# Two role adapters in a row: first loads in chunks on two queues, the up phase's last results on VectorE, and the second layer's first x turned six pairs ahead

## The chip, the cores and the metric

The kernel runs on one core of a Trainium2 chip. A core has five engines that each work through their own list of instructions in order: PE (matrix products), VectorE (DVE), ScalarE (ACT), GpSimd (POOL) and SyncE (SP, which here only issues transfers). ACT can issue transfers too. The metric is the time of one execution on the device in microseconds, lower is better. Before the change it is 3129.63 us, the median of 3 runs (3129.15 to 3130.18).

## What is computed

There are 128 samples, each a matrix of 128 rows by 1024 values, and each has a role, which is one of three. Two layers follow one another. In each layer every sample passes through an adapter whose weights belong to its role:

```python
h = jnp.einsum('bsh,bhk->bsk', hidden_states, W_down[role]) + b_down[role][:, None, :]
h = jax.nn.gelu(h, approximate=False)
u = jnp.einsum('bsk,bkh->bsh', h, W_up[role]) + b_up[role][:, None, :]
y = hidden_states + u
mean = jnp.mean(y, axis=-1, keepdims=True)
var = jnp.mean(jnp.square(y - mean), axis=-1, keepdims=True)
yn = (y - mean) * jax.lax.rsqrt(var + LN_EPS)
return yn * gamma[role][:, None, :] + beta[role][:, None, :]
```

Here the width is 1024 and the inner width 512, all in float32. The second layer has weights of its own and the same roles.

## The kernel before

**Phases and items.** There are four phases: down and up of layer 0, then down and up of layer 1. A phase works through 64 items of two samples each. The samples are sorted on the chip by role, the commonest role first, so that 63 of the items ("pairs") have one role for both samples; one item takes the two samples left over. Below, an item is called by its number m in the phase's order, 0 to 63.

**Products.** A pair is one 2 by 2 block product by Winograd's scheme, with seven block products instead of eight. They use the weight blocks B11, B21, T2, T1, T3, B22, T4 in this order (`ORDER`); the T are differences of blocks. On the other side stand x (turned, so that its columns lie on the partitions) and three sums of its blocks, made by `winograd_sums` in four instructions (L418 to L421), nearly always on GpSimd. One block product takes PE about 1.72 us, a pair 12.06 us. The very first item multiplies plainly (`plain`), because its weights come in as plain rows. Every tensor that is multiplied is brought in by transfers of quarters (`quartered`) and turned by VectorE (`turn`, L547 for x; L656 for the up phases' h).

**The end of an up item.** `finish` normalizes each of the two samples: `squares` (ACT, then a power on GpSimd, L794), `scaled` (VectorE, L801), `stored` and `away`. `stored` multiplies by the deviation's inverse and adds beta: for sample 0 on ACT (L808) and GpSimd (L809), for sample 1 on VectorE (L811). `away` lets SP store the result to `mid` (L815) for the next layer.

**Order.** The order of each engine's instructions is fixed by a list of events with time keys. One item has 7 units (`SLOTS`), so item m of phase k has base 7 * (64 k + m); an event at base + 3.1 comes ahead of one at base + 5.4, and equal keys go in the order in which they were entered. Whatever an event issues, on any engine, stands on that engine's list in the order of the keys and is executed in that order. A key is not a time of execution. Consecutive items overlap: item m + 1 begins between the fourth and the fifth product of item m.

At the seam of the first up phase (k = 1) and the second down phase (k = 2) these keys count, given from the base of the second down phase's item 0:

| key | event | engine |
|---|---|---|
| -15, -14.9 | x of item 0, samples 0 and 1 (eight transfers) | SP |
| -10.6, -8.6 | `squares` of up item 61, samples 0 and 1 | ACT, GpSimd |
| -7.5 | `stored` of up item 61, sample 0 (L808, L809) | ACT, GpSimd |
| -6.9, -3.5 | turns of item 0; at the second one also its sums | VectorE, GpSimd |
| -5.2 | `away` of up item 61, sample 0 | SP |
| -4.9, -4.8 | x of item 1 (eight transfers) | SP |
| -4.4 | `away` of up item 61, sample 1 | SP |
| -4.25, -2.25, -0.25 | weights T2, T1, T3 of the down phase | SP |

The weight blocks live in eight slots of `wall`, each with three parts for the three places of roles. One slot is always spare, and the next phase's B11 goes there. The first three items of the second down phase keep their x in parts of weight blocks that are still empty (`among_weights`).

**The start.** `role_0`, the commonest role, is known first. Its down weights come as rows, 1 MiB by ACT's queue (`load_rows(0, ...)`) and 1 MiB by SP's (`load_rows(1, ...)`), with x of the first sample on SP between the two. Products with zeros (`zeros`, L262) are put between PE's small products of the sorting. `perm`, `role_of` and `place` are gathered by one small product each (`gathered`, L338). `first_sum` makes the differences T1 to T4 in place on VectorE (L171).

```python
at(-31, lambda: load_rows(0, 0, nc.scalar))
at(-30.5, load_bias_row)
at(-29, lambda: load_rows(1, 0, nc.sync))
at(-26, lambda: load_bias([0], nc.scalar))
at(0.3, lambda: subtract(slice(0, 1)))
for t, name in zip((-8.7, -2.5, 4.6, 4.7), ("T1", "T2", "T3", "T4")):
```

Of the kernel before, what the change touches and what calls it, by code (L numbers as in the profile page):

```python
# [13 lines left out]
ALU = mybir.AluOpType  # L14
# [12 lines left out]
def kernel(  # L27
# [117 lines left out]
    def load_rows(k, place, queue):  # L145
        role = reg(role_of, place, [queue.engine], R - 1) if place else reg(role_0, 0, [queue.engine], R - 1)
        src = layers[0][0][ds(role, 1)].rearrange("o (p m) c -> p (o m) c", p=P)
        queue.dma_start(rows_of[k][:, place].rearrange("p j h c -> p j (h c)"), src[:, ts(k, NQ)])

    first_weights = {  # L150
# [142 lines left out]

    zeros("bbbbbbbb")
    role_row, key = ps[:, 0:B], f32(R)
# [47 lines left out]
    perm = gathered("perm", wide, onehot)  # L343
    zeros("bbb")

# [11 lines left out]

    own_place, wide_place = f32(1), f32(SQ)
    counted(own_place, key, own_key, ALU.is_gt, ones_r)
    nc.vector.tensor_copy(wide_place, own_place.to_broadcast((P, SQ)))  # L360
    place = gathered("place", wide_place, onehot)
    zeros("bbbb")

# [9 lines left out]
    def set_places(item, engines):  # L373

        n = item.n
        if n < NFIRST:
            item.places = [0, 0]
        elif n < NPAIR:
            item.places = [reg(place, 2 * n, engines, R - 1)] * 2
        else:  # L380
            item.places = [reg(place, 2 * n + s, engines, R - 1) for s in range(2)]

# [15 lines left out]

    def quartered(t, srcs):

        for s, src in enumerate(srcs):
            n = src.shape[-1] // NQ
            for q in range(NQ):
                nc.sync.dma_start(  # L404
                    t[s][ts(q, SQ)], src[:, ts(q, n)].rearrange("(a t) c -> t a c", t=SQ)
                )
# [110 lines left out]
    class Down:  # L517
# [6 lines left out]

        def load(self):
            if self.among_weights:


                block = self.ph.weights[ORDER[self.m]].v
                self.xq = [block[:, 1 + s] for s in range(2)]  # L530
            else:
                self.xq = [flat("q", 4, f"xq{self.tag}_{s}", H) for s in range(2)]
            self.xq = [t.rearrange("p (a c) -> p a c", a=NQ) for t in self.xq]
            if self.early:
                quartered(self.xq[0:1], [self.early_x(0, ENG.SP)])
                return
            self.srcs = x_of(self.layer, self.n, ENG.SP)
            quartered(self.xq[0:1], self.srcs[0:1])

        def load_rest(self):  # L540
            quartered(self.xq[1:2], [self.early_x(1, ENG.SP)] if self.early else self.srcs[1:2])

# [17 lines left out]
        def prepare(self):  # L560
            self.begin_turns()
            self.sums = None
# [6 lines left out]
        def end_turns(self):  # L569
            if self.early:  # L570
                return
            self.turn(1)
            if self.n < NPAIR:
                winograd_sums(self.sums, self.a, nc.vector if self.ph is phases[0] and self.m == 1 else nc.gpsimd)

        def plain(self):
# [16 lines left out]
            steps = [(4 * s + 2 * k, lambda s=s, k=k: half(s, k)) for s in range(2) for k in range(2)]  # L593
            return steps + [(0.1 + k / 10, lambda k=k: self.turn(1, ts(k, NQ))) for k in range(2)]

# [27 lines left out]
    class Up:  # L623
# [150 lines left out]
        def finish(self):  # L774
            if self.last:
                return self.finish_last()
            steps = []
            for s in range(2):
                t = (10.4, 12.4)[s] if self.n < NPAIR else (10.9, 12.65)[s]
# [39 lines left out]

                steps += [(t, squares), (t + 1.3, scaled)]  # L820


# [21 lines left out]
    for k, ph in enumerate(phases):  # L844
        for m, n in enumerate(sequence):
# [4 lines left out]
            def load(box=box, ph=ph, n=n, kind=kind, m=m):  # L850
# [4 lines left out]
                item.before_last = ph is phases[-1] and m == NI - 2  # L855
                item.among_weights = ph is phases[2] and m < 3
                if m == left_over_at + 1:
                    item.SEED = -1.65
# [24 lines left out]
            if ph is phases[2] and m < 3:  # L883

                prepare = -6.9
                at(base - 3.5, lambda box=box: box["item"].end_turns())
            at(base + prepare, go)
        if k + 1 < len(phases):
# [44 lines left out]
            for name, (slot, free) in zip(ORDER, places):  # L933
# [21 lines left out]
    ph.bias, load_bias, subtract = bias_table(ph.vectors[0], 2)  # L955

    def load_bias_row():
        r = reg(role_0, 0, [ENG.Activation], R - 1)
        nc.scalar.dma_start(bias_row, ph.vectors[0][ds(r, 1), :])
# [58 lines left out]
```

## Time and profile before

The profile is of one execution that took 3130.06 us. Its span, from the first to the last instruction, is 3128.3 us, at a granted TensorE clock of 0.999 on average.

| engine | busy us | share of the span |
|---|---|---|
| PE (products) | 3112.7 | 99% |
| PEld (weight loads, beside the products) | 2047.8 | 65% |
| VectorE | 1975.8 | 63% |
| ScalarE | 1203.5 | 38% |
| GpSimd | 1777.3 | 57% |

Transfers moved 642.21 MB, 205 GB/s on average. A row of the timeline has the start and the length in us, the engine, the line, the operation, what it writes and reads, and how often; in brackets stands the idle time of the engine just before, and what ended it. `SPq` and `ACTq` are transfers issued by SP and ACT. A count in an `x8` is of instructions that ran one after another and are shown as one row. In a float32 product each block of weights takes two instructions.

The page's slices show how the load of VectorE grows in the up phases (each digit is a tenth of busy time in one fortieth of the span):

```profile
DVE  6554544544678777777864444444447877777777
```

The up phases are the slices 10 to 19 and 30 to 39, counted from 0.

### The profile page before, as it was taken

The page shows a single profiled execution, that of the slowest core. Times are in us where ns is not written, and L with a number is a line of the kernel's source. Part 1 is how long each engine was busy: PE and PEld are TensorE (multiplying, and loading weights), DVE is VectorE, ACT ScalarE, POOL GpSimd, SP SyncE. Part 2 cuts the span into 40 slices and gives each one's busy share as a digit, 9 for nine tenths or more (in the row PEclk, how much of TensorE's full clock was granted, in tenths as well). Part 3 has the DMA queues.
Part 4 walks back from the last instruction along what each step waited for, and adds up shares of the span by engine and source line. Part 5 has one row for each costly group of instructions (what it writes and reads, how often), then busy time and mean ns, then how long its engine had stood idle before and what let it go on. Part 6 is the DMA issues. An engine that isn't in the chain of part 4 may idle for free.

```text
span 3128.3 us, 42229 instructions
## 1 busy us (share of the span) xinstructions
PE 3112.7 (99%) x10796; PEld 2047.8 (65%) x10796; DVE 1975.8 (63%) x2807; ACT 1203.5 (38%) x2816; POOL 1777.3 (57%) x1391
## 2 busy tenths in 40 slices
PE   9999999999999999999999999999999999999999
PEld 6888888888544444444478888888884444444443
DVE  6554544544678777777864444444447877777777
ACT  1222222222454555454432222222224545454544
POOL 3545344444577767777654343444436777677775
PEclk9999999999999999999999999999999999999999
DMA  8778788876786565656687555555567765656564
GB/s 218 196 216 209 212 206 210 213 209 196 272 288 240 211 227 208 225 212 226 225 224 179 146 130 131 130 127 138 126 183 275 280 239 206 227 207 226 211 227 176
DMA packets 429735, 642.21 MB, mean 205 GB/s; under 512 B 35778, under 2 KB 305603, under 8 KB 428356
## 3 DMA queue, kind: packets, MB, share of 16 engines
q1 hardware_dynamic: 428930, 637.15, 66.2%
q8 instruction: 102, 1.67, 0.2%
q10 hardware_dynamic: 578, 2.36, 0.2%
q14 instruction: 125, 1.02, 0.1%
HBM read 405.02 MB, written 234.36 MB: 204 GB/s over the span
## 4 chain that ended last, share of the span: by engine, by line
PE 49%; POOL 1%; issue 0%; DMA 0%; SPq 0%; DVE 0%; ACT 0%; DVEq 0%; POOLq 0%; ACTq 0%
PE bu L427 14%; PE bd L427 14%; PE eu L427 7%; PE ed L427 7%; PE au L427 3%; PE ad L427 3%; POOL ou L809 0%; SPq L404 0%; DMA hd<-hd 0%; POOL Sd L420 0%; POOL Sd L418 0%; DMA wall<-mid 0%; POOL varu L794 0%; POOL xTd L419 0%; DVE ou L712 0%
## 5 line engine op out<-in xcount | busy, mean ns | idle before, releaser
L427 PE MATMUL bu<-wall,hTu 128*128 (+1 forms) x2048 | 921.3, 592 | 0.0
L547 DVE STREAM_TRANSPOSE xTd<-xqd 128x1024 f32<-128x1024 f32 (+1 forms) x252 | 504.9, 2071 | 350.7 <-PE bd L427 283.8
L427 PEld LDWEIGHTS bu<-wall,hTu 128*128 128x128 f32 x2048 | 389.1, 190 | 487.2 <-issue 456.6
L418 POOL TENSOR_TENSOR Sd<-xTd 128x512 f32<-128x512 f32 x124 | 159.7, 1288 | 790.4 <-DVE xTd L547 782.7
L794 POOL TENSOR_TENSOR varu<-varu,mhalf 128x1 f32<-128x1 f32 x254 | 329.6, 1298 | 393.8 <-ACT varu L793 393.8
L427 PE MATMUL bd<-wall,xTd 128*128 (+1 forms) x2064 | 487.1, 379 | 1.8 <-ACT bd L445 1.8
L427 PE MATMUL eu<-wall,hTu 128*128 (+1 forms) x1040 | 488.0, 592 | 0.0
L427 PE MATMUL bd<-wall,Sd 128*128 (+1 forms) x2000 | 472.8, 379 | 2.2 <-ACT hd L606 1.6
L427 PEld LDWEIGHTS bd<-wall,xTd 128*128 128x128 f32 x2064 | 392.0, 190 | 57.5 <-ACT bd L445 2.6
L427 PEld LDWEIGHTS bd<-wall,Sd 128*128 128x128 f32 x2000 | 379.7, 190 | 56.5 <-issue 2.6
L801 DVE SCALAR_TENSOR_TENSOR ou<-xu,meanu,tables 128x1024 f32<-128x1024 f32 x253 | 325.3, 1286 | 138.3 <-ACT ou L792 120.0
L611 ACT ACTIVATE hd<-hd 128x256 f32<-128x256 f32 x379 | 157.6, 416 | 534.5 <-DVE hd L610 534.4
L427 PEld LDWEIGHTS eu<-wall,hTu 128*128 128x128 f32 x1040 | 197.6, 190 | 247.4 <-issue 218.8
L788 ACT ACTIVATE partu<-statu 128x2 f32<-128x2 f32 x254 | 51.6, 203 | 728.7 <-DVE xu L690 728.7
L809 POOL TENSOR_TENSOR ou<-ou,tables 128x1024 f32<-128x1024 f32 x126 | 296.9, 2356 | 0.0
L792 ACT ACTIVATE ou<-xu,meanu 128x1024 f32<-128x1024 f32 x254 | 291.7, 1148 | 8.4
L681 DVE TENSOR_TENSOR xu<-bu,xu 128x512 f32<-128x512 f32 x256 | 176.1, 688 | 119.1 <-PE bu L427 119.1
L427 PE MATMUL ed<-wall,xTd 128*128 (+1 forms) x1064 | 251.0, 379 | 0.0
L418 POOL TENSOR_TENSOR hTu<-hTu 128x256 f32<-128x256 f32 x126 | 198.1, 1572 | 70.8 <-DVE hTu L656 49.0
L427 PE MATMUL au<-wall,hTu 128*128 (+1 forms) x504 | 236.8, 592 | 0.0
L427 PE MATMUL ed<-wall,Sd 128*128 (+1 forms) x1000 | 236.3, 379 | 0.1
L427 PE MATMUL ad<-wall,xTd 128*128 (+1 forms) x1000 | 236.2, 379 | 0.0
(135 smaller groups left out, 3383.1 us busy)
## 6 DMA issues: line engine op xcount, KB each, us to landing
xqd<-in_x_dram SPq DMA_DIRECT2D x512, 128.0 KB, 3.3
hd<-hd SPq DMA_DIRECT2D x256, 256.0 KB, 2.4
xu<-in_x_dram SPq DMA_DIRECT2D x128, 512.0 KB, 3.8
mid<-ou SPq DMA_DIRECT2D x128, 512.0 KB, 4.2
xu<-mid SPq DMA_DIRECT2D x128, 512.0 KB, 3.8
out_dram<-ou SPq DMA_DIRECT2D x125, 512.0 KB, 3.8
hqu<-hd SPq DMA_DIRECT2D x244, 256.0 KB, 5.0
xqd<-mid SPq DMA_DIRECT2D x488, 128.0 KB, 3.8
```

What stands on the lines that cost most here:

```text
L418: engine.tensor_tensor(dst[:, 1], a11, a21, ALU.subtract)
L427: nc.tensor.matmul(ps[:, 0:cols], a[:, j], w.rhs(r, j, cols), start=start and j == 0, stop=j == n - 1, skip_group_check=True,)
L547: nc.vector.transpose(self.a[:, s, chunks].rearrange("p j (t a) -> p j a t", t=SQ), self.xq[s].rearrange("p a (i j) -> p j a i", i=SQ)[:, ...
L611: nc.scalar.activation(y, y, AF.Gelu)
L681: nc.vector.tensor_tensor(y, ps, y, ALU.add)
L788: nc.scalar.mul(part, self.stat[:, s], -1.0 / H)
L792: nc.scalar.activation(box["o"], self.x[:, s], AF.Square, bias=m, accum_out=v)
L794: nc.gpsimd.tensor_tensor(v, v, mhalf[:, 0:1], ALU.pow)
L801: nc.vector.scalar_tensor_tensor(box["o"], self.x[:, s], box["m"][:, 0:1], row(self.ph.gamma), ALU.add, ALU.mult)
L809: nc.gpsimd.tensor_tensor(o, o, row(self.ph.beta), ALU.add)
```

## The change

Five things are done, in two groups.

At the start:
1. The first role's rows come in eight chunks of 256 KiB (`load_first_rows`), the first on ACT, then by turns on SP and ACT, the last on ACT; `first_role` keeps the role's register. x of the first sample goes half by SP and half by ACT, between the first and the second chunk.
2. `zeros` has 14 products instead of 8 behind the row of roles and 4 instead of 3 behind `perm`. `place` and the four zeros behind it leave the sorting: `own_places` goes to VectorE behind the first turns, and the gather comes behind the first half of the first sample's product. The turn of sample 1, `subtract` and T2 get later keys.

At the seam:

3. Item 0 of the second down phase is `ahead`. Its x is loaded one sample at a time (keys -42 and -31.5) into part 0 of the spare slot and turned into parts 1 and 2 (keys -34.8 and -24.3). The spare slot has B11's part 0 loaded later, as before; parts 1 and 2 of the weight blocks of this phase are loaded in another order, B11's last. Its sums get the key -8.4.
4. For up items 62 and 63 of layer 0 (`ending`) `stored` is on VectorE for both samples, at key t + 2.5 instead of t + 3.1.
5. For these two items `away` has the key t + 3.6 (before, t + 5.4 and t + 4.2).

```diff
+    def load_first_rows(j, queue):
+        src = rows_in_dram(first_role(queue.engine))
+        queue.dma_start(rows_of[j // NQ][:, 0, j % NQ].rearrange("p h c -> p (h c)"), src[:, j])
...
-    zeros("bbbbbbbb")
+    zeros("bbbbbbbbbbbbbb")
...
-    zeros("bbb")
+    zeros("bbbb")
...
-    own_place, wide_place = f32(1), f32(SQ)
-    counted(own_place, key, own_key, ALU.is_gt, ones_r)
-    nc.vector.tensor_copy(wide_place, own_place.to_broadcast((P, SQ)))
-    place = gathered("place", wide_place, onehot)
-    zeros("bbbb")
+    own_place, wide_place, place = f32(1), f32(SQ), []
+    def own_places():
+        counted(own_place, key, own_key, ALU.is_gt, ones_r)
+        nc.vector.tensor_copy(wide_place, own_place.to_broadcast((P, SQ)))
+    def places_in_order():
+        place.append(gathered("place", wide_place, onehot))
...
         def load(self):
+            if self.ahead:
+                self.srcs = x_of(self.layer, self.n, ENG.SP)
+                self.a = self.ph.weights[ORDER[0]].v[:, 1:3].rearrange("p s (j c) -> p s j c", c=P)
+                return
...
             if self.early:
-                quartered(self.xq[0:1], [self.early_x(0, ENG.SP)])
+                for k, queue in enumerate((nc.sync, nc.scalar)):
+                    quartered(self.xq[0:1], [self.early_x(0, queue.engine)], (2 * k, 2 * k + 1), queue)
...
+        def load_ahead(self, s):
+            self.xq = [self.ph.weights[ORDER[0]].v[:, 0].rearrange("p (a c) -> p a c", a=NQ)] * 2
+            quartered(self.xq[s : s + 1], self.srcs[s : s + 1])
...
-            return steps + [(0.1 + k / 10, lambda k=k: self.turn(1, ts(k, NQ))) for k in range(2)]
+            return steps + [(1.1 + k / 10, lambda k=k: self.turn(1, ts(k, NQ))) for k in range(2)]
...
+            ending = self.layer == 0 and self.m >= NI - 2
...
-                    if s == 0 and not self.before_last:
+                    if s == 0 and not self.before_last and not ending:
...
+                if ending:
+                    steps += [(t + 2.5, stored), (t + 3.6, away)]
+                    continue
...
+            elif m == 0:
+                first = rest = -43
+                for s in range(2):
+                    at(base - 42 + 10.5 * s, lambda box=box, s=s: box["item"].load_ahead(s))
+                    at(base - 34.8 + 10.5 * s, lambda box=box, s=s: box["item"].turn(s))
             else:
-                first = -15 if m == 0 else -11.9
+                first = -11.9
...
-                prepare = -6.9
-                at(base - 3.5, lambda box=box: box["item"].end_turns())
+                prepare = -6.9 if m else -8.5
+                at(base - 3.5 if m else base - 8.4, lambda box=box: box["item"].end_turns())
...
-                    later_on = SLOTS * (1 + 2 * ORDER.index(name) + k_)
+                    turn = ORDER.index(name) if nxt.up else (ORDER.index(name) - 1) % len(ORDER)
+                    later_on = SLOTS * (1 + 2 * turn + k_)
...
-    at(-31, lambda: load_rows(0, 0, nc.scalar))
+    at(-31, lambda: load_first_rows(0, nc.scalar))
     at(-30.5, load_bias_row)
-    at(-29, lambda: load_rows(1, 0, nc.sync))
+    for j in range(1, 7):
+        at(-29 + j / 10, lambda j=j: load_first_rows(j, nc.sync if j % 2 else nc.scalar))
+    at(-27, lambda: load_first_rows(7, nc.scalar))
     at(-26, lambda: load_bias([0], nc.scalar))
-    at(0.3, lambda: subtract(slice(0, 1)))
-    for t, name in zip((-8.7, -2.5, 4.6, 4.7), ("T1", "T2", "T3", "T4")):
+    at(-8.75, own_places)
+    at(1, places_in_order)
+    at(2.7, lambda: subtract(slice(0, 1)))
+    for t, name in zip((-8.7, 2.6, 4.6, 4.7), ("T1", "T2", "T3", "T4")):
```

More of the change, by code (lines that the diff above doesn't have):

```diff
@@ L1 @@
+import functools
 import heapq
@@ L145, in load_rows, with rows_in_dram @@
     def load_rows(k, place, queue):
-        role = reg(role_of, place, [queue.engine], R - 1) if place else reg(role_0, 0, [queue.engine], R - 1)
-        src = layers[0][0][ds(role, 1)].rearrange("o (p m) c -> p (o m) c", p=P)
+        src = rows_in_dram(reg(role_of, place, [queue.engine], R - 1))
         queue.dma_start(rows_of[k][:, place].rearrange("p j h c -> p j (h c)"), src[:, ts(k, NQ)])
+    def rows_in_dram(role):
+        return layers[0][0][ds(role, 1)].rearrange("o (p m) c -> p (o m) c", p=P)
+    def load_first_rows(j, queue):
+        src = rows_in_dram(first_role(queue.engine))
+        queue.dma_start(rows_of[j // NQ][:, 0, j % NQ].rearrange("p h c -> p (h c)"), src[:, j])
     first_weights = {
@@ L378, in set_places @@
         elif n < NPAIR:
-            item.places = [reg(place, 2 * n, engines, R - 1)] * 2
+            item.places = [reg(place[0], 2 * n, engines, R - 1)] * 2
         else:
-            item.places = [reg(place, 2 * n + s, engines, R - 1) for s in range(2)]
+            item.places = [reg(place[0], 2 * n + s, engines, R - 1) for s in range(2)]
     def samples(n, engine):
@@ L397, with quartered @@
     bias_row = first_rows[0:1, 0]
-    def quartered(t, srcs):
+    def quartered(t, srcs, quadrants=range(NQ), queue=nc.sync):
         for s, src in enumerate(srcs):
             n = src.shape[-1] // NQ
-            for q in range(NQ):
-                nc.sync.dma_start(
+            for q in quadrants:
+                queue.dma_start(
                     t[s][ts(q, SQ)], src[:, ts(q, n)].rearrange("(a t) c -> t a c", t=SQ)
@@ L538, in load @@
             quartered(self.xq[0:1], self.srcs[0:1])
+        def load_ahead(self, s):
+            self.xq = [self.ph.weights[ORDER[0]].v[:, 0].rearrange("p (a c) -> p a c", a=NQ)] * 2
+            quartered(self.xq[s : s + 1], self.srcs[s : s + 1])
         def load_rest(self):
+            if self.ahead:
+                return
             quartered(self.xq[1:2], [self.early_x(1, ENG.SP)] if self.early else self.srcs[1:2])
@@ L560, in prepare @@
         def prepare(self):
-            self.begin_turns()
+            if not self.ahead:
+                self.begin_turns()
             self.sums = None
@@ L571, in end_turns @@
                 return
-            self.turn(1)
+            if not self.ahead:
+                self.turn(1)
             if self.n < NPAIR:
@@ L856, in load @@
                 item.among_weights = ph is phases[2] and m < 3
+                item.ahead = ph is phases[2] and m == 0
                 if m == left_over_at + 1:
@@ L955, with first_role @@
     ph.bias, load_bias, subtract = bias_table(ph.vectors[0], 2)
+    @functools.cache
+    def first_role(engine):
+        return reg(role_0, 0, [engine], R - 1)
     def load_bias_row():
-        r = reg(role_0, 0, [ENG.Activation], R - 1)
-        nc.scalar.dma_start(bias_row, ph.vectors[0][ds(r, 1), :])
-    at(-31, lambda: load_rows(0, 0, nc.scalar))
+        nc.scalar.dma_start(bias_row, ph.vectors[0][ds(first_role(ENG.Activation), 1), :])
+    at(-31, lambda: load_first_rows(0, nc.scalar))
     at(-30.5, load_bias_row)
-    at(-29, lambda: load_rows(1, 0, nc.sync))
+    for j in range(1, 7):
+        at(-29 + j / 10, lambda j=j: load_first_rows(j, nc.sync if j % 2 else nc.scalar))
+    at(-27, lambda: load_first_rows(7, nc.scalar))
     at(-26, lambda: load_bias([0], nc.scalar))
-    at(0.3, lambda: subtract(slice(0, 1)))
-    for t, name in zip((-8.7, -2.5, 4.6, 4.7), ("T1", "T2", "T3", "T4")):
+    at(-8.75, own_places)
+    at(1, places_in_order)
+    at(2.7, lambda: subtract(slice(0, 1)))
+    for t, name in zip((-8.7, 2.6, 4.6, 4.7), ("T1", "T2", "T3", "T4")):
         at(t, lambda name=name: first_sum(name, 0))
```

## The prediction

> **What bounds the kernel now.** I read the page first. PE is busy 99% of a span of 3128.3 us and the chain that ended last is PE from end to end, so a gain can only come from the few places where PE waits. The list of waits gives PE some 10 us of them; laying PE's starts one after another (429 ns from one 512-column product to the next, 216 ns for 256 columns) puts nearly all the loss at three places: the start, the seam between the first up phase and the second down phase, and the tail, which the change leaves alone.
>
> The start, as stretches of the trace (length, PE, PEld, DVE, ACT, POOL busy, granted clock, DMA share, GB/s), then as a timeline:
>
> ```profile
> 12.29:15.70 3.41, 2.43 (x8) 0.83 (x6) 1.91 (x3) 0.00 (x0) 0.00 (x0) 1.00 0.98 329
> 15.70:19.11 3.41, 3.41 (x6) 1.34 (x5) 2.57 (x3) 0.00 (x0) 0.00 (x0) 0.50 1.08 233
> ...
> 13.84 2.13 DVE L547 STREAM_TRANSPOSE xTd<-xqd 128x512 f32<-128x512 f32 x2 [1.50 <-DMA xqd<-in_x_dram]
> 15.02 8.83 PE L587 MATMUL ad<-wall,xTd 128*128 128x512 f32 x16 [0.98 <-DVE xTd L547]
> 20.64 2.14 DVE L547 STREAM_TRANSPOSE xTd<-xqd 128x512 f32<-128x512 f32 x2 [2.33 <-DMA xqd<-in_x_dram]
> 24.84 7.13 PE L587 MATMUL ad<-wall,xTd 128*128 128x512 f32 x16
> ```
>
> PE has its first real product at 15.02 because sample 0's x lands only at 13.7; then it runs one stretch of 3.41 us at half clock. Starts spaced 0.53 to 0.85 us instead of 0.43 cost 1.8 us there.
>
> The seam, PE's timeline:
>
> ```profile
> 1568.16 1.97 PE L427 MATMUL bd<-wall,Sd 128*128 128x256 f32 x8 [0.49 <-DMA wall<-T]
> 1574.15 1.99 PE L427 MATMUL bd<-wall,xTd 128*128 128x256 f32 x8 [0.57 <-ACT bd L445]
> 1589.07 1.99 PE L427 MATMUL bd<-wall,xTd 128*128 128x256 f32 x8 [1.21 <-ACT bd L445]
> 1597.50 1.96 PE L427 MATMUL bd<-wall,Sd 128*128 128x256 f32 x8 [1.26 <-ACT hd L606]
> ```
>
> With three smaller ones these gaps sum to 5.9 us between 1567 and 1598. Behind those named ACT stands VectorE: it turns x four times between 1554 and 1576, and two adds of beta (L811) take 3.36 us instead of 1.25 because GpSimd's L809 runs at the same moment.
>
> GpSimd and SP's queue just before it are what I find decisive:
>
> ```profile
> 1552.58 1.32 POOL L794 TENSOR_TENSOR varu<-varu,mhalf 128x1 f32<-128x1 f32 x1 [2.45 <-ACT varu L793]
> 1553.87 2.38 POOL L809 TENSOR_TENSOR ou<-ou,tables 128x1024 f32<-128x1024 f32 x1
> 1561.33 0.55 POOL L794 TENSOR_TENSOR varu<-varu,mhalf 128x1 f32<-128x1 f32 x1 [5.08 <-ACT varu L793]
> ...
> 1550.52 0.32 SPq L937 DMA_DIRECT2D wall<-B  x1
> 1556.28 0.32 SPq L815 DMA_DIRECT2D mid<-ou  x1
> 1556.65 5.07 SPq L404 DMA_DIRECT2D wall<-mid  x8
> 1561.82 0.38 SPq L815 DMA_DIRECT2D mid<-ou  x1
> 1562.30 2.03 SPq L937 DMA_DIRECT2D wall<-T  x3
> ```
>
> SP stands still from 1550.84 until L809 of item 61, sample 0, ends (1556.25); only then go its store, item 1's eight x loads and the load of T2, which PE awaits at 1568.16. T2 is late already, by 0.5 us, and all of it hangs on that one GpSimd instruction.
>
> **The start.** Ahead of x stand 256 KiB of rows instead of 1 MiB; 0.79 MB less at the 0.36 MB/us that the trace moved from 8 to 10 us is 2.2 us. Two queues: the four issues take 2.15 us on SP (6.29 to 8.44); with half on ACT, behind a row chunk, the bias row and a register load, the last goes out near 7.9, 0.5 us sooner. A rule speaks against this part: the Trainium skill, "DMA: Bandwidth & Descriptors", section "Issuing engines are not separate DMA queues", says that the queues share the same engines, so a second one saves issue time alone. By it and by the row the queue is worth 0.5 us; what counts is the order of the bytes. x lands near 11.0, half a turn (1.07) makes PE ready at 12.3; the bias product (1.12 us, now right behind the last zeros) ends at 12.8. Real start 12.8 for 15.02: 2.2 us. PE has no hole ahead of it, since six more zeros (0.26 each) and one more fill it, so the half clock should go: 1.8 us. The place gather now lies inside the sample: 0.4 us back (L338, x2). Sum 3.6 us.
>
> What is late next: sample 1's x (turn at 20.64) has to be turned by 21.2; if it lands no sooner than now, its first half ends at 21.7, and 3.1 us remain. Item 2's turn (32.82 to 34.84, behind item 1's x, landed at 25.2, the sums and T3, T4) would let item 2 start at 34.95 for 38.71 now: a cap of 3.7. The row chunks have 2 KiB runs instead of 8 KiB. In the trace 8 KiB packets took 383 to 405 ns here; 2 KiB ones 150 ns (the bias table at 12 to 17 us) or 85 (300 to 400 us). Between, 110 ns: 2.1 MB take 7.0 us instead of some 6.4. DMA is full until 33 us, so this shifts all that follows. I take **3.4 us gained**, ends 0.5 (150 ns, the rival below) and 3.7. T2's moved difference (1.23 us) follows the turn on VectorE and is wanted only at item 1's third product.
>
> **x of the second down phase, six pairs ahead.** Its eight x loads go from one burst to two of four (some 2 us of SP each); hidden. The two turns (2.1 us each) leave 1554 and 1559 and go into pair items 59 and 60 on VectorE, which is 9.47 us busy per 12 there. How VectorE answers to an inserted 2 us the trace shows, at L916:
>
> ```profile
> 1504.17 0.69 DVE L690 SCALAR_TENSOR_TENSOR xu<-bu,xu 128x512 f32<-128x512 f32 x1 [0.19 <-PE bu L427]
> 1515.92 2.49 DVE L916 TENSOR_TENSOR first_rows<-first_rows 128x256 f32<-128x256 f32 x1
> 1518.33 0.68 DVE L690 SCALAR_TENSOR_TENSOR xu<-bu,xu 128x512 f32<-128x512 f32 x1
> 1530.07 0.68 DVE L690 SCALAR_TENSOR_TENSOR xu<-bu,xu 128x512 f32<-128x512 f32 x1
> ```
>
> PE's period is 12.06. The second L690 is 2.1 us late, the third still 1.8: a delay stays, since VectorE then waits 1.27 us twice per item for ACT. So the first turn leaves 1.8 us of lag, L916 adds its own, and the second turn, of which 1.27 us fill such a wait, 0.7. Lag against before: 2.4 us. At its height the second turn stands ahead of item 60's third result, now read at 1522.55: 1522.55 + 1.8 + 2.1 + 0.7 = 1527.1. PE wants that bank four slots of 1.72 us after the third product began (1519.3), at 1526.2: **1.0 us of new wait** with the hand-over (0 to 1.5).
>
> **Its sums on GpSimd.** Their key moves to -8.4. In issue order that is behind the power of item 61's sample 1 (-8.6) and ahead of L809 of item 61's sample 0 (-7.5). Four of 1.27 us with gaps are 5.35 us; beside VectorE's two-input work the four took 7.2 at 1561.85; I take 6.4, since the L811 and L801 in that stretch cross them. L809 then ends at 1556.25 + 2.4 + 6.4 + some 0.2 = 1565.3 instead of 1556.25. Item 61 is not among those whose end goes to VectorE, so its store really waits for it. SP's order behind it is unchanged: store, eight loads, store, T2. T2 lands 11.8 us after that store now (1556.25 to 1568.05), so at 1577.1. PE reaches that product at 1567.5 + 1.0 = 1568.5 and waits **8.6 us** instead of 0.65; with fewer waits of SP among the eight loads (4.15 us in the next burst, not 5.07) 7.7. I take 8.2; with no lag at all 5.9.
>
> Such a hole has a price after it. The same skill, "TensorE: Matmul & The Clock Gate", Part 1, says that an idle window of about 3.4 us halves the clock until a busy one has passed. One window at half is 1.7 us; by the row above a window 71% busy still led to one at 0.50, so it may be 2.7 us. I take **1.7**.
>
> **The end of the up phase on VectorE.** Items 62 and 63 lose two ACT multiplies (1.13) and two L809 (2.36); VectorE gains two of 1.25 us, but its two L811 fall from 3.36 to 1.25: -1.7 us. With the turns gone and PE held at T2, VectorE and ACT are ahead afterwards: the waits at 1574 to 1597 go. The whole 5.9 us is taken off, since the T2 wait is counted anew.
>
> **Sum:** -3.4 + 1.0 + 8.2 + 1.7 - 5.9 = +1.6 us. The sum is made against the profiled execution (3130.06: its span and 1.8 us around); the median shown is 0.4 below it. 3129.63 + 1.6 = **3131.2**. Its own range, from the ends (no lag: -1.3; start 2.5, wait 9.3, clock 2.7: +5): 3127 to 3135.
>
> **Rivals.** (1) T2 is not held: the sums slip in before 1553 or SP is not the gate. Then -3.4 - 5.9 + 1.0 + some 0.6 of the old T2 wait = -7.7: 3122. For it: GpSimd idles 5 us at 1556. Against: each engine keeps its order, and SP stands exactly until L809. Chance 0.15.
> (2) Slower: the 2 KiB rows at 150 ns. 2.1 MB take 9.6 us instead of 6.4, item 1's x lands at 28.4, item 2's turn ends near 38 and the start is worth 0.5 us; with the rest unchanged +4.5: 3134. It decides once a 2 KiB packet takes over about 120 ns. Chance 0.2.
> (3) The wait does not cool the clock and there is no lag: 3128 or less; inside the first case.
> The forecast has 0.65. That the change does something else than it says I see no way to; the order of issue is fixed by its keys.
>
> A measurement of this kernel tells about 0.2%, 6.3 us, from no change: below 3123.4 is faster, above 3135.9 slower. Faster 0.14, nearly all of rival 1; slower 0.18 from the upper part of rival 2 and of the main case; same 0.68. Range 3124 to 3136.5.
>
> **What would show it.** With the start's gain all times are some 3.4 us earlier. Right: first L587 product near 12.8, no clock of 0.50 before 20 us; GpSimd with four L418 to L421 between L794 and the last L809 of the phase; SP's mid store some 9 us later; one PE wait of 6 to 9 us for wall<-T and a slice at half clock behind it; no other wait above 0.3 us up to 1600; PE's hole near 1523. Wrong: T2 issued near 1559, or the first item 1 product later than 29.

## The result, and the profile after

The changed kernel takes 3138.5 us (median of 9 runs, eight of them at 3137.0 to 3139.1), the kernel before beside it 3129.71 (9 runs, 3128.08 to 3131.95): **slower by 0.28%** (ratio 1.0028, 95% interval 1.0019 to 1.0036). The ninth run took 3216.4 us, at a granted clock of 0.972 where the others have 0.997 or 0.998, and is left out of the ratio. Forecast were 3131.2 us and a range up to 3136.5. The profiled execution took 3139.03 us with a span of 3137.2, 8.9 longer than before.

Two places differ. The first rows below are windows of the changed kernel: start and end, length, then busy time of PE, PEld, DVE, ACT, POOL (counts in brackets), granted clock, share of the DMA engines in use and GB/s.

```profile
11.60:15.01 3.41, 1.81 (x5) 0.73 (x5) 1.86 (x2) 0.00 (x0) 0.00 (x0) 1.00 1.05 331
15.01:18.43 3.42, 3.42 (x6) 1.34 (x5) 1.69 (x5) 0.00 (x0) 0.00 (x0) 0.50 1.06 249
...
1571.48:1574.90 3.42, 0.00 (x0) 0.00 (x0) 2.06 (x2) 0.00 (x0) 0.00 (x0) 1.00 1.06 253
1574.90:1578.31 3.41, 0.00 (x0) 0.00 (x0) 3.41 (x8) 1.17 (x5) 0.00 (x0) 0.50 1.05 393
1578.31:1581.72 3.41, 2.65 (x6) 2.19 (x7) 2.50 (x2) 1.48 (x3) 1.82 (x2) 0.50 0.98 368
1581.72:1585.14 3.42, 3.42 (x6) 1.69 (x5) 0.00 (x0) 0.37 (x1) 3.25 (x3) 0.50 1.06 349
1585.14:1588.55 3.41, 3.41 (x16) 2.81 (x15) 2.08 (x4) 1.92 (x5) 1.27 (x1) 1.00 1.14 218
```

The half clock of the start is still there, and the seam has got one of its own, three windows long. The timeline of VectorE and PE at the start, after the change (the code has moved: L571 is the turn, L613 and L438 are products, L456 copies the bias into a bank, L707 and L716 read results, L179 makes the differences):

```profile
13.15 2.12 DVE L571 STREAM_TRANSPOSE xTd<-xqd 128x512 f32<-128x512 f32 x2 [2.03 <-DMA xqd<-in_x_dram]
14.34 5.40 PE L613 MATMUL ad<-wall,xTd 128*128 128x512 f32 x8 [1.59 <-DVE xTd L571]
21.95 2.13 DVE L571 STREAM_TRANSPOSE xTd<-xqd 128x512 f32<-128x512 f32 x2 [1.57 <-DMA xqd<-in_x_dram]
24.68 7.13 PE L613 MATMUL ad<-wall,xTd 128*128 128x512 f32 x16
39.94 2.00 PE L438 MATMUL bd<-wall,xTd 128*128 128x256 f32 x8 [1.21 <-ACT bd L456]
```

x of sample 0 is there 0.7 us sooner, that of sample 1 is 1.3 us later (21.95 for 20.64), and item 2 begins at 39.94 for 38.71. The start loses 1.2 us where 3.4 were to be won.

The seam, first PE, then GpSimd (L822 the power, L429 to L432 the sums, L837 the beta add), VectorE and SP's queue (L843 the store to `mid`, L415 item 1's x, L974 weights):

```profile
1528.25 1.98 PE L438 MATMUL bu<-wall,hTu 128*128 x4 [0.47 <-DVE xu L707]
...
1569.50 1.96 PE L438 MATMUL eu<-wall,hTu 128*128 x4 [1.01 <-DVE xu L707]
1579.07 3.75 PE L438 MATMUL bd<-wall,Sd 128*128 128x256 f32 x8 [7.62 <-DMA wall<-T]
```

```profile
1556.16 1.32 POOL L822 TENSOR_TENSOR varu<-varu,mhalf 128x1 f32<-128x1 f32 x1 [2.44 <-ACT varu L821]
1557.46 1.26 POOL L429 TENSOR_TENSOR Sd<-wall 128x512 f32<-128x512 f32 x1
...
1563.59 3.33 POOL L837 TENSOR_TENSOR ou<-ou,tables 128x1024 f32<-128x1024 f32 x1
1566.88 2.28 POOL L822 TENSOR_TENSOR varu<-varu,mhalf 128x1 f32<-128x1 f32 x2
```

```profile
1567.47 1.28 DVE L839 SCALAR_TENSOR_TENSOR ou<-ou,varu,tables 128x1024 f32<-128x1024 f32 x1 [2.14 <-POOL varu L822]
1568.67 0.68 DVE L707 TENSOR_TENSOR xu<-eu,xu 128x512 f32<-128x512 f32 x1
```

```profile
1553.05 0.32 SPq L974 DMA_DIRECT2D wall<-B  x1
1566.95 0.32 SPq L843 DMA_DIRECT2D mid<-ou  x1
1567.32 4.16 SPq L415 DMA_DIRECT2D wall<-mid  x8
1571.58 0.38 SPq L843 DMA_DIRECT2D mid<-ou  x1
1572.05 2.36 SPq L974 DMA_DIRECT2D wall<-T  x3
```

Read upwards: PE waits 7.62 us for T2; SP issues T2 at 1572.05, because it stood from 1553.4 until the store of item 61 at 1566.95; that store waits for L837, and L837 stands behind the four sums. The other waits after 1573 are gone. The wait of 1.01 us ahead of it is new: VectorE stands at item 62's `stored` (L839) for the power on GpSimd, which is behind L837 too, and PE's result is read behind that.

Below, a kernel's **offset** is how much later than in the kernel before PE starts one and the same product, trace against trace. Of the changed kernel it is +1.33 us at 75 us (all of the start) and +8.74 at 1606 us, and it stays there to the end. So in this trace the start costs 1.33 us and the seam 7.41.

### The profile page after: what moved, and what is told of

Same layout as the page of the kernel before. It is cut to its first block, busy times and chain, and to the rows that moved or that the text cites. A ratio compares the mean times of both kernels' runs of the same rounds, so it can differ in the third digit from the quotient of the medians.

```text
span 3137.2 us, 42253 instructions
## 1 busy us (share of the span) xinstructions
PE 3115.6 (99%) x10799; PEld 2049.8 (65%) x10799; DVE 1974.9 (63%) x2809; ACT 1201.9 (38%) x2814; POOL 1772.1 (56%) x1389
## 3 DMA queue, kind: packets, MB, share of 16 engines
q8 instruction: 102, 1.67, 0.2%
## 5 line engine op out<-in xcount | busy, mean ns | idle before, releaser
L438 PE MATMUL bu<-wall,hTu 128*128 (+1 forms) x2048 | 922.9, 593 | 0.7 <-DVE xu L707 0.7
L571 DVE STREAM_TRANSPOSE xTd<-xqd 128x1024 f32<-128x1024 f32 (+1 forms) x252 | 505.9, 2072 | 350.5 <-PE bd L438 282.9
L438 PEld LDWEIGHTS bu<-wall,hTu 128*128 128x128 f32 x2048 | 389.5, 190 | 489.3 <-issue 455.2
L429 POOL TENSOR_TENSOR Sd<-xTd 128x512 f32<-128x512 f32 x123 | 157.5, 1280 | 795.1 <-DVE xTd L571 795.1
L822 POOL TENSOR_TENSOR varu<-varu,mhalf 128x1 f32<-128x1 f32 x254 | 330.2, 1300 | 398.9 <-ACT varu L821 398.7
L438 PE MATMUL eu<-wall,hTu 128*128 (+1 forms) x1040 | 488.1, 592 | 1.0 <-DVE xu L707 1.0
L438 PE MATMUL bd<-wall,xTd 128*128 (+1 forms) x2048 | 483.3, 379 | 1.2 <-ACT bd L456 1.2
L438 PE MATMUL bd<-wall,Sd 128*128 (+1 forms) x2000 | 474.3, 380 | 7.6 <-DMA wall<-T 7.6
L438 PEld LDWEIGHTS bd<-wall,xTd 128*128 128x128 f32 x2048 | 389.0, 190 | 55.7 <-ACT bd L456 1.6
L438 PEld LDWEIGHTS bd<-wall,Sd 128*128 128x128 f32 x2000 | 381.0, 191 | 61.3 <-issue 9.4
L438 PEld LDWEIGHTS eu<-wall,hTu 128*128 128x128 f32 x1040 | 197.5, 190 | 248.8 <-issue 218.8
L837 POOL TENSOR_TENSOR ou<-ou,tables 128x1024 f32<-128x1024 f32 x124 | 293.2, 2364 | 0.0
L707 DVE TENSOR_TENSOR xu<-bu,xu 128x512 f32<-128x512 f32 x256 | 175.9, 687 | 118.4 <-PE bu L438 118.4
L438 PE MATMUL ed<-wall,xTd 128*128 (+1 forms) x1056 | 249.1, 379 | 0.0
L429 POOL TENSOR_TENSOR hTu<-hTu 128x256 f32<-128x256 f32 x126 | 197.7, 1569 | 72.8 <-DVE hTu L682 60.6
L438 PE MATMUL au<-wall,hTu 128*128 (+1 forms) x504 | 236.8, 592 | 0.0
L438 PE MATMUL ed<-wall,Sd 128*128 (+1 forms) x1000 | 236.2, 379 | 0.0
L438 PE MATMUL ad<-wall,xTd 128*128 (+1 forms) x992 | 234.3, 379 | 0.0
```

Source lines behind the costliest of these rows:

```text
L429: engine.tensor_tensor(dst[:, 1], a11, a21, ALU.subtract)
L438: nc.tensor.matmul(ps[:, 0:cols], a[:, j], w.rhs(r, j, cols), start=start and j == 0, stop=j == n - 1, skip_group_check=True,)
L571: nc.vector.transpose(self.a[:, s, chunks].rearrange("p j (t a) -> p j a t", t=SQ), self.xq[s].rearrange("p a (i j) -> p j a i", i=SQ)[:, ...
L707: nc.vector.tensor_tensor(y, ps, y, ALU.add)
L822: nc.gpsimd.tensor_tensor(v, v, mhalf[:, 0:1], ALU.pow)
L837: nc.gpsimd.tensor_tensor(o, o, row(self.ph.beta), ALU.add)
```

## The experiments

All ratios are against the kernel before, run on the same chip in the same rounds (median 3128.7 to 3129.2 us). "Seam" is PE's lost time between 1490 and 1620 us: 5.9 us before, 13.3 in the changed kernel.

### Which half of the change costs what

`e1_start_alone` has parts 1 and 2 of the change on the kernel before, `e2_seam_alone` parts 3 to 5.

> Only the start's part of the change, on the kernel before. By PE's starts the start costs 1.2 us (item 2's first product at 39.94 for 38.71), so 3131 us. Rival, that start and seam need each other (the earlier or later start shifts what happens at the seam): then anything away from +1.2 by over 2 us. My forecast's own term was -3.4 us, 3126.

> Only the seam's part, on the kernel before. By PE's starts waits and half clock at the seam grow from 5.9 to 13.3 us, so +7.4 us, 3137 us, with the one wait of some 7.7 us for wall<-T. If the seam is worth less without the new start, the two parts meet somewhere.

Measured: the start alone 3133.02 us (1.0014, 1.0007 to 1.0020), offset +2.35 at 75 us; the seam alone 3134.93 us (1.0019, 1.0011 to 1.0027), seam 11.8 us, offset +5.93 at the end. Each is a loss of its own, and the start is no gain that something later takes back. By the medians the halves cost 4.2 and 6.1 us, the whole change 8.8; the start alone is 2 us above what was expected for it. The start does not cost the same in every execution: the five traces with exactly this start have offsets at 75 us of +1.33 (the changed kernel), +1.75 (e4 below), +2.35 (e1), +3.93 (e10) and +4.18 (e3). In the last two item 2 waits 2.2 us instead of 1.21, and another window at half clock follows, from 41.3 and 42.0 us.

### What holds T2 at the seam

Three ways to free it, each on the changed kernel. In `e3_sums_behind` the sums go behind the beta add on GpSimd:

```diff
-                at(base - 3.5 if m else base - 8.4, lambda box=box: box["item"].end_turns())
+                at(base - 3.5 if m else base - 7.4, lambda box=box: box["item"].end_turns())
```

In `e4_weights_first` T2, T1 and T3 are loaded ahead of item 61's store:

```diff
-                at(base + free + 0.75, lambda f=load_part: f(0))
+                early = {"T2": 1.7, "T1": 1.71, "T3": 1.72} if k == 1 else {}
+                at(base + early.get(name, free + 0.75), lambda f=load_part: f(0))
```

In `e10_store_behind_weights` only item 61's stores move, behind those three loads; the sums keep their place:

```diff
-                    steps.append((t + (5.4, 4.2)[s], away))
+                    late = self.layer == 0 and self.m == NI - 3
+                    steps.append((20.8 + s / 20 if late else t + (5.4, 4.2)[s], away))
```

> The changed kernel with the four sums of item 0 behind L809 of item 61 on GpSimd (key -7.4 for -8.4). Theory of the queue: L809 ends some 5.6 us sooner, SP's store, x of item 1 and T2 with it; PE waits about 2 us for T2 in place of 7.8 and the clock stays full: 9 to 10 us less than the changed kernel, 3128 to 3129.5. Rival, the lag of VectorE from the two turns is what costs: the wait stays over 6 us, under 3 us gained.

> The changed kernel with the sums where it has them (L809 just as late), but T2, T1 and T3 are put on SP's queue ahead of item 61's store and of item 1's x. Theory of the queue: T2 lands near 1560, no wait for wall<-T, no half clock; what is left are the waits at 1527, 1533 and 1568 and perhaps 1 us for item 1's x: 8.5 to 10.5 us less than the changed kernel, 3128 to 3130. Rival, the lateness of GpSimd itself (sums, L809, the powers behind it)[...] holds PE: at most 3 us gained.

> The changed kernel with nothing moved but SP's two stores of up item 61, from keys -5.2 and -4.4 to -0.2 and -0.15: behind the loads of T2, T1 and T3. The sums still stand ahead of the beta add on GpSimd, which still ends near 1567. If SP's queue behind that store is what holds T2 (my theory): T2 is issued before 1563, PE's wait of 7.6 us for it and the half clock behind it go, the lag of 1.2 us and the wait of 1.25 us at 1568 stay, and the time falls by 6 to 10 us against the changed kernel (some 3130). If GpSimd's delay holds PE in another way (the sums themselves, the buffers of the results): a wait of several us stays at the seam and the time stays above 3135.

Measured: e3 3132.82 us (1.0012, 1.0003 to 1.0021), seam 5.6 us. e4 3135.77 (1.0021, 1.0014 to 1.0029), seam 8.1. e10 3132.79 (1.0011, 1.0004 to 1.0018), seam 5.6. PE and SP in e10:

```profile
1572.14 1.96 PE L438 MATMUL eu<-wall,hTu 128*128 x4 [1.02 <-DVE xu L707]
1573.93 1.89 PE L438 MATMUL bd<-wall,Sd 128*128 128x256 f32 x8
1576.98 1.98 PE L438 MATMUL bu<-wall,hTu 128*128 x4 [1.16 <-DVE xu L716]
...
1562.96 3.34 SPq L975 DMA_DIRECT2D wall<-T  x3
1569.59 2.15 SPq L843 DMA_DIRECT2D mid<-ou  x3
```

The beta add (1566.23 to 1569.57) is as late as ever and the store too, but T2 is issued at 1562.96, its product has no wait, and the half clock is gone with the wait. So SP's queue is the gate, as was argued. What comes then is the next thing in line: waits of 1.16 us at 1577 and 1.41 at 1591 for VectorE, which the long wait had covered. With T2 free the seam is thus 5.6 us, hardly under the 5.9 before. In time e3 and e10 are 5.7 us below the changed kernel, less than the 9 to 10 and the 6 to 10 that were expected, although their seams are 7.7 us shorter: their starts cost 2.9 and 2.6 us more in the traces.

e4 did not show this, because its edit made a wait of its own: T2's slot still had a reader, the second product of item 63 (`au`). The load is entered ahead of that product, so the product waits for it.

```profile
1560.17 3.55 PE L438 MATMUL au<-wall,hTu 128*128 x4 [5.00 <-DMA wall<-T]
```

### The lag of VectorE, and the end of the up phase

On the kernel before, with the old start: `e5_ahead_without_ending` has x six pairs ahead and its sums at -7.4, but `ending` off; `e6_ending_without_ahead` has the three `ending` hunks of `finish` alone; `e7_turns_in_waits` has the whole seam part with the sums at -7.4 and other keys for loads and turns. First e5's line (beside that of e3), then e7's:

```diff
-            ending = self.layer == 0 and self.m >= NI - 2
+            ending = False
```

```diff
-                first = rest = -43
+                first = rest = -46
...
-                    at(base - 42 + 10.5 * s, lambda box=box, s=s: box["item"].load_ahead(s))
-                    at(base - 34.8 + 10.5 * s, lambda box=box, s=s: box["item"].turn(s))
+                    at(base - 45.5 + 7.5 * s, lambda box=box, s=s: box["item"].load_ahead(s))
+                    at(base - 38.3 + 7 * s, lambda box=box, s=s: box["item"].turn(s))
```

> Old start. x of the second down phase turned ahead, its sums behind L809 of item 61, but items 62 and 63 end as before (sample 0 on ACT and GpSimd). If it is the turns in the crowded stretch that made the old 5.9 us of waits, they fall to some 1.2 us at 1526 and 1532 and about 3 us at the seam: 3128, 1 us less than before. If the end of the items made them[...], they stay near 5.9 and the 1.2 come on top: 3130.

> The kernel before with nothing but the new end of items 62 and 63 (sample 0's last step on VectorE). [...]both L811 fall from 3.36 to about 1.3 us, VectorE is some 1.7 us less behind and the waits at 1574 to 1597 fall from 5.2 to 3 us: 3127. If only the turns matter, no change: 3129. If the new step waits for GpSimd's power and holds what stands behind it on VectorE, as at 1567 in the changed kernel, slower by 1 to 2 us.

> Old start, the whole seam part with the sums behind L809, and the two turns put where VectorE waits for ACT anyway (keys -38.3 and -31.3, in two items ahead of L916's). Theory of the lag: VectorE is not behind when L916 comes, so the waits of 1.2 us at 1526 and 1532 are gone, L809 ends 2 us sooner than with the turns at -34.8 and -24.3, and the seam has 3 to 4.5 us of waits: 3126.5 to 3128.5. Rival, any 4 us more on VectorE in the up phase come out as lag: the waits stay, 3129.5 to 3130.5.

Measured: e5 3128.49 us (0.9998, 0.9990 to 1.0007), seam 4.6; e6 3128.34 (0.9998, 0.9989 to 1.0007), seam 4.8; e7 3127.32 (0.9994, 0.9986 to 1.0003), seam 4.5. None can be told from no change, so here the traces decide. PE at the place of the lag, e5 and then e7:

```profile
1526.90 1.99 PE L427 MATMUL bu<-wall,hTu 128*128 x4 [0.48 <-DVE xu L694]
...
1532.56 2.81 PE L427 MATMUL bu<-wall,hTu 128*128 x6 [0.24 <-DVE xu L694]
```

```profile
1523.05 3.60 PE L427 MATMUL bu<-wall,hTu 128*128 x8
...
1529.96 3.67 PE L427 MATMUL bu<-wall,hTu 128*128 x8
...
1565.57 1.96 PE L427 MATMUL eu<-wall,hTu 128*128 x4 [1.02 <-DVE xu L694]
```

With the turns where VectorE waited for ACT anyway, both waits (1.0 us together) are gone: the lag was real. The seam is hardly shorter than in e5, since others have come. The wait at 1565.57 stays in e7 and is absent from e5, so it comes from the `ending` part: item 62's `stored`, moved up on VectorE, waits for a power that GpSimd has no time for. Not all of e7's lower time is the seam's: its trace has no half clock at the start, which the edit leaves as it was, so its offset is -1.5 us at 75 us already and -2.9 at the end.

### Why the start loses

`e8_T2_before_turn`, on e1, puts T2's difference back ahead of sample 1's turn:

```diff
-    for t, name in zip((-8.7, 2.6, 4.6, 4.7), ("T1", "T2", "T3", "T4")):
+    for t, name in zip((-8.7, -2.5, 4.6, 4.7), ("T1", "T2", "T3", "T4")):
```

`e9_more_zeros` is the kernel before with more zeros behind `place`:

```diff
     place = gathered("place", wide_place, onehot)
-    zeros("bbbb")
+    zeros("bbbbbbb")
```

`e11_three_chunks` and `e13_long_runs` are e1 with the rows cut in other ways. The first has 256 KiB, then 768 KiB on ACT and 1 MiB on SP; the second has eight times 256 KiB as in e1, but 32 partitions at a time:

```diff
-    for j in range(1, 7):
-        at(-29 + j / 10, lambda j=j: load_first_rows(j, nc.sync if j % 2 else nc.scalar))
-    at(-27, lambda: load_first_rows(7, nc.scalar))
+    at(-28.9, lambda: load_first_rows(1, nc.scalar))
+    at(-28.8, lambda: load_first_rows(4, nc.sync))
```

```diff
-        queue.dma_start(rows_of[j // NQ][:, 0, j % NQ].rearrange("p h c -> p (h c)"), src[:, j])
+        k, part = j // NQ, ts(j % NQ, SQ)
+        queue.dma_start(rows_of[k][part, 0].rearrange("p j h c -> p j (h c)"), src[part, ts(k, NQ)])
```

> The start's part alone, with T2's difference back ahead of sample 1's turn (key -2.5). If the wait of item 2 (1.5 us in the start alone) comes from VectorE's list, the 1.2 us of T2 fall into VectorE's wait for x and item 2 begins 1.2 us sooner: about 3132 for 3133. If x of sample 1 and the bytes ahead of it set it alone, no change against the start alone; if T2's own rows come last (they landed at 19.6 to 20.5) and hold the turn, no change or slower.

> The kernel before with three more products with zeros behind place (seven instead of four). They fill 0.78 us of PE's hole between 13.0 and 15.0 us. If the window of half clock from 15.7 to 19.1 us is there only because PE stands still ahead of the first product: no row at 0.50 before 20 us, sample 1's first product near 23.0 instead of 24.8, and 1.0 to 1.7 us less in all (some 3127.5), since item 2 can start only as soon as its turned x allows, 0.85 us after which it starts now. If the half clock comes from something else: it stays, and the time is that of the kernel before within 0.5 us.

> The start of the changed kernel alone (as in e1_start_alone), with the first role's rows in three transfers instead of eight: the first 256 KiB on ACT as there, then 768 KiB on ACT in runs of 6 KiB and 1 MiB on SP in runs of 8 KiB. If the short runs and the many transfers are what brings sample 1's x later (22.7 to 23.2 us in that start, 19.8 to 20.6 in the old one): its turn starts by 20.8, item 2 waits less than 0.5 us, and the time is that of the kernel before or up to 2 us below it (3127 to 3129). If the order of the bytes is what does it, whatever the size of the pieces: the turn still starts after 22, item 2 still waits over 1 us, and the time is 3131 to 3133.

> The start of the changed kernel alone (as in e1_start_alone), its eight transfers of 256 KiB kept in number, size, queue and order, but cut by partitions (32 at a time, runs of 8 KiB) instead of by rows (all 128, runs of 2 KiB). If the short runs are what makes sample 1's x late: a MB costs some 3.7 us of the engines' time again instead of 3.98, its turn starts at 21.5 or sooner, item 2 waits under 1.0 us, and the time is 3129 to 3131.5. If the number and order of transfers do it: the turn starts at 22.3 or later as in e1 and e8, and the time is 3132 to 3133.5. The first product can come later in either case (15 or 16 us), since each product needs rows on all partitions, so four transfers instead of one.

Measured (turns' starts and the first product of item 2 in us, offset at 75 us):

| kernel | median us, ratio (interval) | turn of sample 0 | of sample 1 | item 2 | offset |
|---|---|---|---|---|---|
| before | | 13.84 | 20.64 | 38.71 | 0 |
| e1 | 3133.02, 1.0014 (1.0007 to 1.0020) | 14.11 | 22.99 | 40.96 | +2.35 |
| e8 | 3132.11, 1.0010 (1.0001 to 1.0019) | 12.83 | 22.70 | 39.83 | +1.22 |
| e11 | 3134.88, 1.0018 (1.0011 to 1.0026) | 16.31 | 23.97 | 42.21 | +3.50 |
| e13 | 3133.48, 1.0015 (1.0009 to 1.0022) | 11.17 | 22.29 | 40.91 | +2.30 |
| e9 | 3129.47, 1.0001 (0.9993 to 1.0009) | 14.07 | 20.39 | 37.76 | -0.85 |

In the six profiles with the new start's loads as they are (the changed kernel, e1, e3, e4, e8, e10) sample 1 is turned at 21.95 to 23.16 us, in the eight with the old ones at 19.75 to 20.64. The ranges do not touch. Windows from 4 us to that turn, of the kernel before, of the changed kernel and of e13:

```profile
4.00:20.64 16.64, 13.27 (x39) 5.04 (x38) 10.68 (x51) 0.00 (x0) 0.00 (x0) 0.90 0.88 234
```

```profile
4.00:21.95 17.95, 15.18 (x46) 5.99 (x45) 9.47 (x49) 0.00 (x0) 0.00 (x0) 0.90 0.85 217
```

```profile
4.00:22.29 18.29, 15.42 (x45) 6.00 (x44) 9.56 (x50) 0.00 (x0) 0.00 (x0) 0.91 0.86 195
```

Length times GB/s is 3.89 MB in the first, 3.90 in the second: the same bytes stand ahead of sample 1's x, but they come at 217 instead of 234 GB/s. By the packets' own times a MB took 3.64 us of all 16 engines on average of the old starts, 3.98 of the new. Up to sample 0's turn the same product gives 2.07 MB before (9.84 us at 210) and 1.67 after (9.15 us at 182): only 0.40 MB less, where 0.79 were counted, because chunks that were issued beside or after x share the engines with it: of the 1.67 MB, x is 0.52 and the rows 1.15, of which only 0.26 were issued ahead of x. e11 shows this at its plainest: with two large transfers issued beside x, 2.72 MB move until x is there, and it is turned at 16.31. Its first product starts only at 17.49, and its time lies above both that were expected. In e13 it is 1.09 MB, and x is turned at 11.17; but there the first product waits for rows until 15.02.

Where the lower rate comes from was the question for e13, and the answer is only half of one. Long runs don't bring it back: its packets of 8 KiB took 569 ns on average, in the kernel before 396, and the turn came at 22.29, between the two expectations and near the second. The packets of 2 KiB in e1 took 120 ns. e11, with three transfers, is back at 3.72 us per MB. So the short runs alone are not the cause, and cutting 2 MiB into eight costs in either way of cutting. Whether the rate falls by the number of transfers, their alternation on two queues or, in e13, the 32 partitions, stays open.

The number of transfers counts in another way, too, and the prediction has no term for it. In the traces all transfers use eight semaphores in turn to tell that they have landed, and an issue stands until the earlier transfer with its semaphore has landed. SP's waits before x (us in total, how often, the longest), from 8 to 16 us in the changed kernel and from 8 to 14 us in the kernel before, in both until sample 1's last quarter is issued:

```profile
SPq L415 <- DMA wall<-in_L_cond_W_down_dram: 3.3, 3, 1.7
SPq L415 <- DMA xqd<-in_x_dram: 0.8, 1, 0.8
```

```profile
SPq L404 <- DMA wall<-in_L_cond_W_down_dram: 1.5, 1, 1.5
SPq L404 <- DMA xqd<-in_x_dram: 0.2, 1, 0.2
```

With more chunks in flight the four quarters of sample 1's x go out at 10.70, 12.87, 14.27 and 15.53, each within 0.02 us of the landing it waits for; before, the last one went out at 13.00. In e13 that is 15.46, in e11 14.75. How much of the 1.3 us comes from the late issue and how much from the rate, no run separates.

What follows from sample 1's late x is a chain on VectorE, in order: turn of sample 1, T2's difference, two turns of item 1, three sums, T3 and T4, two turns of item 2, and only then the L636 of item 1 for which ACT and then PE wait (39.94 in the rows above). In the kernel before this chain had 0.85 us of slack (ACT's L445 ended at 37.86, item 2 began at 38.71); after, it is 2.0 us later. e8 takes T2's 1.2 us out of it again: from the turn of sample 1 to the first turn of item 1 it takes 2.3 us (22.70 to 25.02), in e1 3.5 (22.99 to 26.45). By its median e8 is 0.9 us faster than e1, by its offset 1.1; but the intervals of the two times overlap and the offset of one start varies by more than that, so it is the rows that show the cost.

e9 has PE busy for 2.85 of the 3.41 us ahead of 15.70, where the kernel before has 2.43:

```profile
12.29:15.70 3.41, 2.85 (x10) 0.98 (x8) 1.69 (x3) 0.00 (x0) 0.00 (x0) 1.00 1.01 330
15.70:19.11 3.41, 3.41 (x9) 1.52 (x8) 2.80 (x3) 0.00 (x0) 0.00 (x0) 1.00 1.09 230
```

There is no half clock, item 1 begins 1.5 us sooner, item 2 0.95 and the offset is -0.85, as expected. But its median is that of the kernel before: in its trace the seam lost 6.5 us instead of 5.9, by longer waits for T2 (1.21 us for 0.65) and at 1597 (2.06 for 1.43), and the end is only 0.27 us earlier. The gain is shown by the trace and not by the times.

Nor are more zeros the only way to a full window. Of the five traces with the old start and no more zeros, four (the kernel before, e2, e5, e6) have 2.32 to 2.47 us of work in the window ahead of the half clock. The fifth, e7, has 2.88 and no half clock:

```profile
12.67:16.08 3.41, 2.88 (x8) 1.08 (x7) 2.69 (x3) 0.00 (x0) 0.00 (x0) 1.00 1.00 338
16.08:19.50 3.42, 3.42 (x10) 1.51 (x9) 1.75 (x2) 0.00 (x0) 0.00 (x0) 1.00 1.01 226
```

There x was turned at 13.39 instead of 13.81 to 13.96, so that more of the first products fall into the window; and the windows begin at another moment in each execution. So whether the old start meets the half clock is in part chance. With the zeros of e9 none of three traces (e9, e12, e14) has it.

### What of it can be kept

`e12_both_mended` has the old start with the zeros of e9, x six pairs ahead with the keys of e7 and `ending = False`. `e14_mended_and_store_behind` adds the late stores of e10.

> The old start with three more zeros (e9), and of the seam only x six pairs ahead, turned inside VectorE's waits (e7) with its sums behind the beta add (e3), and the up phase's end as before. If the parts add: 1.0 to 1.7 us from the start, the lag of 1.0 us of e5 gone, seam excess near 3.5 us instead of 5.9: 3125 to 3126.5, below both kernels. If something takes back what each gives, it is within 0.5 us of 3128.5 as e5 was.

> e12_both_mended with SP's two stores of up item 61 behind the loads of T2, T1 and T3, as in e10. If that store holds SP there too (it waits for GpSimd's beta add, near 1556): PE's wait of 0.79 us at 1566 goes and the time is 0.5 to 1 us below e12 (some 3126.3). If T2 is late for another cause (its slot, the transfers ahead of it): the wait stays and the time is that of e12 within 0.4 us.

Measured: e12 3127.07 us (0.9994, 0.9985 to 1.0002), seam 4.1, offset -1.15 at 75 us (e7 had -1.5 without the zeros) and -2.96 at the end. e14 3127.12 (0.9994, 0.9986 to 1.0002), offset -3.32. In e14 T2's wait is gone and smaller ones have come behind it: the seam is 4.1 us again, and the 0.36 us by which its offset is lower are there at 75 us already. So that store does hold T2 there, and freeing it is worth nothing. Both are some 11 us below the changed kernel; against the kernel before they are 2 us below by the medians and 3 by the traces, which the times alone cannot tell from nothing.

## Why the prediction was wrong, point by point

**The step that failed is the start's term: -3.4 predicted, +1.33 in the trace of the changed kernel, +1.2 to +4.2 in the six traces with this start.** It fails at three places of its working.

- "Ahead of x stand 256 KiB of rows instead of 1 MiB": x was put at 11.0 and came at 13.0. In transfers that run at once, what counts is not what was issued ahead of x (0.26 MB of rows) but what moves until it lands (1.15 MB of rows). The first product came at 14.34, not 12.8. The second queue did what was said: the last quarter of x went out at 7.85, for 7.9.
- "PE has no hole ahead of it, so the half clock should go": the bias product did move up (11.62 to 12.74), but x didn't, so the hole grew to 1.6 us and the half clock stayed, in all six.
- Sample 1's x "no sooner than now" was taken as the worst case; it came 1.3 to 2.5 us later, issued later and moved at a lower rate. And the price of T2's difference behind the turn was set at nothing, since its product is far; it stands in VectorE's chain for item 2, and costs some 1.1 us there (e8's rows).

Rival 2 pointed the right way and named the packets; its limit of about 120 ns is just where e1's packets lay. But it kept 0.5 us of gain for the start, and the start loses.

**The seam's term was right in its mechanism and too small.** Predicted were 1.0 + 8.2 + 1.7 - 5.9 = 5.0 us; the offset grew by 7.41.

- T2's wait: 8.2 predicted, 7.8 measured from start to start, and e10 shows the chain from the beta add over SP to T2. The store went out 9.3 us later than before once the start's 1.33 is taken off.
- The lag: 1.0 predicted, 1.2 measured (waits at 1527 and 1533), and e7 removes it.
- The half clock behind it: 1.7 predicted for one window, 3.1 measured. "TensorE: Matmul & The Clock Gate", Part 1, in the Trainium skill gives one idle window as the cause and one busy one as the way back. The rows agree on the first (a window with no product, then 0.50), though at the start a window with 1.82 us of work had the same effect; and on the second only if the busy window has to be filled: the window with 2.65 us of work was followed by one more at 0.50.
- The waits of 5.9 us: all gone, as said, and the adds of beta on VectorE behind the seam take 1.24 to 1.28 us, where two took 3.36. In their place came 1.2 us at 1568, not foreseen: the price on GpSimd was followed to the beta add and to SP, but not to the power behind it, for which VectorE waits, now earlier than before by the `ending` part.

The two errors went the same way: 4.7 us at the start and 2.4 at the seam are the 7.1 us by which 8.74 exceeds 1.6.

Of the signs listed, four were right (sums between the power and the beta add; the store some 9 us late; one wait of 6 to 9 us for T2 with a half clock behind it; PE's hole near 1523), three wrong (first product, no clock of 0.50 before 20, no other wait above 0.3 us: there were 1.01 at 1569.50 and 0.47 at 1528.25), and the line "first item 1 product later than 29" had named the failure: it came at 31.65.

Some small sums and readings in it are off, and none of them makes the failure. Without lag the wait for T2 would be 8.2 - 2.4 + 1.0 = 6.8 us and not 5.9, since PE comes 1.0 us sooner too, and the lower end -0.8 us and not -1.3; the upper end comes to +4.6 and not +5. "DMA is full until 33 us" does not hold from 24 to 31 us, where its share is 0.86 and then 0.73.

## What to carry to other kernels

Splitting a load so that the urgent part comes first gains only if the rest is not in flight with it: count what moves until the urgent part has landed, at the rate that the smaller pieces reach, look when the transfers behind it can be issued at all, and follow the engine that turns it as one chain to the next item. When a step is put ahead of another in an in-order queue, list everything behind that other, to the end of the next queue too: here four additions on GpSimd cost 7.8 us over a store and a load on SP. A place made free shows the next wait, so a wait taken away is worth less than its length.

## What was not expected of the hardware

- How full a window must be to keep the clock is not told by PE's busy time alone, as the table shows. One count puts the windows of all 16 traces in order, up to 30 us before the end: leave out the products with a single row of weights (those of the bias, and one of the sorting), and let work at half clock count half. Windows with up to 1.42 us by this count were followed by one at 0.50, windows with 1.48 us or more by one at 1.00. The count was found after the runs, and no run was made to test it.

| trace, start of the window | PE busy, us | clock in it | by the count, us | next clock |
|---|---|---|---|---|
| before, 12.29 | 2.43 | 1.00 | 1.38 | 0.50 |
| e2, 11.88 | 2.47 | 1.00 | 1.42 | 0.50 |
| changed kernel, 1578.31 | 2.65 | 0.50 | 1.32 | 0.50 |
| e10, 14.02 | 2.97 | 0.50 | 1.48 | 1.00 |
| before, 5.46 | 1.71 | 1.00 | 1.71 | 1.00 |
| e9, 12.85 | 2.85 | 1.00 | 1.80 | 1.00 |
| e7, 12.67 | 2.88 | 1.00 | 1.84 | 1.00 |

- The hole at T2 was 7.6 us long and the half clock behind it lasted 10.24 us, some 6 of them over running products.
- Packets of the same 8 KiB took 396 ns on average in transfers of 1 MiB over all 128 partitions and 569 ns in transfers of 256 KiB over 32 partitions.
